# Norm scale moved into the qkv eviction, fills of v ahead of the sets, both columns ahead of choice: three edits in an eight-layer kernel

## The chip, the cores and the metric

The kernel runs on one core of one Trainium2 chip, as one program launched once. The metric is the time of one execution on the device, in microseconds; lower is better. The engines are called by the names that the profile uses: PE for the matmul engine, PEld for its weight loads, DVE for the vector engine, ACT for the scalar engine, POOL for GpSimd, SP for the engine that issues most transfers. All data is fp32. An fp32 matmul instruction stands in the trace as two records.

## The reference

The input is x of shape (8, 256, 256), that is 2048 tokens of width 256. It goes through four groups of three layers; each group is a half-weighted feed-forward layer, an attention, and the same feed-forward layer again:

```python
x = x + 0.5 * ffn_n(layernorm(x))
x = x + attn_n(layernorm(x))
x = x + 0.5 * ffn_n(layernorm(x))      # n = 0, 1, 2, 3
```

Every feed-forward layer is a shared gated product for all tokens and a choice of 2 of 7, 8, 16 or 8 experts for each token. The second attention (n = 1), which the change touches most, is

```python
qkv = rms(x) @ w_qkv.T; q, k, v = split(qkv)      # x is the normed input
q = rms(q); k = rms(k); w = exp(k)
y = sigmoid(q) * cumsum(w * v) / (cumsum(w) + 1e-6)
u, g = split(y @ w_swiglu.T)
out = x + u * silu(g) @ w_out.T
```

where rms(x) is x times the inverse root of the mean of its squares plus EPS1. Its input is already the layernorm of the stream, so its own rms scale is close to, but not exactly, one. The result contains the normed input once more (the leading x). The third attention (n = 2) is causal softmax attention with 32 heads of width 8 and biases on q, k, v and the output.

## The kernel before, in words

The 2048 tokens are 16 tiles of 128 (`NT`), held in SBUF as `net.x[i]`, and four blocks of four tiles (`NB`). A block is the unit of all stages. The function `moments` (L292) takes a block's mean and variance with four pairs of bn_stats and bn_aggr on DVE (L298, L299) and a square root on ACT (L269 and L270 in `root`). `norm_rows` (L304) inverts the root and forms minus mean times scale on DVE (L306, L308), and writes the normed rows on ACT (L310) into `net.rows`, one buffer for all 16 tiles. `to_columns` (L277) transposes four row tiles on PE (L284, two banks with the tag "t") and copies the halves out, the first on DVE and the second on ACT (both L285), to `hT`, which the products read.

A feed-forward layer is an object of the class `Sparse`. `norm` writes its rows, `columns` (L817) transposes them and computes the routing logits (L829, turned back at L843, copied out by DVE at L841 and L850), `choose` (L864) picks two experts by some twenty small DVE operations that end with L898, and `place` (L923) counts with two small matmuls (L932, L933), computes each token's slot on DVE (L937 to L952, the slot's cast is L950), and has POOL scatter the block's rows to DRAM, `sent`, one indirect transfer to a tile (L961). The experts fetch their tokens from there as `got` and turn them on PE (L1077). Their results go back with indirect transfers (`back`), and `combine` (L1141, eight DVE operations a block at L1149, reading `mine`) adds them to x. The shared product runs in `glu_steps`: matmuls L351 into banks "up", an activation L355 or L358 on ACT, a product L364 on DVE, matmuls L369 into "y", and the addition L376 to x on DVE.

`Sparse.body` (L1230) is one pass through such a layer. It calls `arrange` with the blocks that are still to be routed, and a generator `beside` that hands out pieces of the shared product: `beside(7)` means, run pieces until their amounts sum to 7. Inside `arrange` PE's order is written by hand: PE issues what the code issues, in that order. The other engines' instructions are put in order by the compiler's scheduler from estimated costs. After the pass over the experts, `body` runs the rest of the shared product and the combines, and after each block's combine calls `after(j)`, which for a first pass is `normed` (L1971): it writes the normed rows of that block for the attention that follows.

An attention then leaves some blocks to the layer behind it. It routes the others itself while its last work runs, and returns the rest: blocks 2 and 3 after the first and the fourth attention, block 3 after the second and the third. These are the blocks that `arrange` gets in the second pass of each layer. In the first pass of the first layer it gets all four, in the first passes of the others none.

The second attention is `attn1` (L1337). For each block it calls `attn1_front` (L1320): POOL adds the normed rows to x (L1328), ACT squares the rows with a sum (L1330), DVE and ACT make the rms scale, DVE scales the rows in place (L1333), and `to_columns` follows. Then for each of four tiles PE computes 768 columns as 512 and 256 (L1356, four banks with the tag "up"), DVE copies both to `qkv` (L1363), and ACT takes the sums of squares of q and k (L1366). These give `r`, the scale of q and k (L270, L275, L1371). After the four blocks comes a scan over the 16 tiles: two exponentials on ACT (`w` L1382, `eq` L1384), a product on POOL (L1385), cumulative sums by matmuls with a triangle and ones (L1389, L1390), and four DVE operations (L1393 to L1397, of which L1395 is a reciprocal).

The third attention is `attn2` (L1635) with the class `HeadTiles` (L1408). Its constructor casts two constants, `eye` (L1432) and `far` (L1430), takes two sets of four zeroed tiles (qs, ks, qm, km; fills on POOL at L1445) and then 16 tiles `v`, filled with ones on POOL (L1454), because one column of each head must be 1. Then for each block q and k are computed (L1655, banks "a" and "b", three each), evicted on ACT with bias (L1657; the scaled bias of q comes from L1646 on DVE), written to DRAM as `qd` and `kd`; the four v products (L1665) go to banks "t" and DVE adds their bias into `v` (L1669). `load(0)` reads the first heads back into set 0, and the scores (L1486) follow. Tiles of these pools lie where tiles of the stage before lay, so that a fill waits until the last reader of what was there is done.

Of the kernel before, what the change touches and what calls it, by code (L numbers as in the profile page):

```python
# [183 lines left out]
class Net:  # L184


    def __init__(self, ctx, tc, io):
        self.tc, self.nc, self.io = tc, tc.nc, io
        nc = self.nc
        self.const = ctx.enter_context(tc.tile_pool(name="const", bufs=1))  # L190
        self.flow = ctx.enter_context(tc.tile_pool(name="flow", bufs=1))
        self.routes = ctx.enter_context(tc.tile_pool(name="routes", bufs=2))
        self.small = ctx.enter_context(tc.tile_pool(name="small", bufs=2))
        self.dram = ctx.enter_context(tc.tile_pool(name="dram", bufs=2, space=DRAM))
        self.psum = None
        self.passes = 0


        self.sent = self.dram.tile([16 * T + 8 * P, ROW], F32, tag="sent", name="sent", bufs=1)
        self.back = self.dram.tile([2 * T + P * max(TILES.values()), D], F32, tag="back", name="back", bufs=1)  # L200
        self.c = {}
        for k in ("ident",):
            self.c[k] = self.constant(self.const, k)
        self.x = []
        self.stream(0, NT // 2)
        for k in ("ids", "prio7", "base7", "ones", "below", "later4"):
            self.c[k] = self.constant(self.const, k)
        self.router = {"f0": self.load(self.const, "f0_r")}
        self.f0_b = self.row(self.const, "f0_b")

        self.rows = self.flow.tile([P, NT, ROW], F32, tag="rows", name="rows")
        self.hT = [None] * NB

    def stream(self, lo, hi):

# [71 lines left out]

    def norm_block(self, j, tiles):

        self.norm_rows(j, tiles, *self.moments(j))  # L290

    def moments(self, j):  # L292

# [468 lines left out]
class Sparse:  # L762
# [389 lines left out]

    def arrange(self, blocks, beside):

        for j in blocks[:2]:
            self.norm(j)
        if 0 < len(blocks) < NB:
            beside(7)
        for i, j in enumerate(blocks):
            self.columns(j)  # L1160
            self.choose(j)
            if i + 2 < len(blocks):
                self.norm(blocks[i + 2])
            beside(5)
            self.place(j)
# [151 lines left out]
EPS1 = 1.1920929e-07  # L1317


def attn1_front(net, j):  # L1320


    nc = net.nc
    tiles = net.row_tiles(j)
    ss = net.small.tile([P, 4], F32, tag="ss", name="ss")
    for q in range(4):
        x = net.x[4 * j + q]
        nc.gpsimd.tensor_tensor(x, x, tiles[q], ALU.add)  # L1328
        junk = net.small.tile([P, D], F32, tag="sq", name="sq", bufs=1)
        nc.scalar.activation(junk, tiles[q], AF.Square, accum_out=ss[:, q : q + 1])  # L1330
    net.rstd(ss, ss, 1.0 / D, EPS1)
    for q in range(4):
        nc.vector.tensor_scalar(tiles[q], tiles[q], ss[:, q : q + 1], None, ALU.mult)  # L1333
    net.hT[j] = net.to_columns(tiles, j)


def attn1(net, w, then):  # L1337
    nc, tc = net.nc, net.tc
    with tc.tile_pool(name="a1", bufs=2, reuse_waits="tile") as pool:
        triu = net.constant(pool, "triu")  # L1340
        ones = net.c["ones"]
        up = net.load(pool, "a1_up", parts=4)
        dn = net.load(pool, "a1_dn", parts=2)
        wqkv = w["a1_qkv"]
        with tc.tile_pool(name="a1k", bufs=1, reuse_waits="tile") as keep:
            qkv, rr = [], []
            for j in range(NB):
                attn1_front(net, j)
                hT = net.hT[j]
                r = keep.tile([P, 8], F32, tag=f"r{j}", name=f"r{j}")  # L1350
                for q in range(4):
                    t = keep.tile([P, 768], F32, tag=f"qkv{4 * j + q}", name=f"qkv{4 * j + q}")
                    for lo, hi in ((0, 512), (512, 768)):
                        ps = net.bank("up", 4)
                        for k in range(KD2):
                            nc.tensor.matmul(  # L1356
                                ps[:, : hi - lo],
                                lhsT=hT[:, k, q * P : (q + 1) * P],
                                rhs=wqkv[:, k, lo:hi],
                                start=(k == 0),  # L1360
                                stop=(k == KD2 - 1),
                            )
                        nc.vector.tensor_copy(t[:, lo:hi], ps[:, : hi - lo])  # L1363
                    for n in range(2):
                        junk = pool.tile([P, D], F32, tag="junk", name="junk")
                        nc.scalar.activation(  # L1366
                            junk, t[:, n * D : (n + 1) * D], AF.Square, accum_out=r[:, 4 * n + q : 4 * n + q + 1]
                        )
                    qkv.append(t)
                net.rstd(r, r, 1.0 / D, EPS1)  # L1370
                nc.vector.tensor_scalar(r[:, 0:4], r[:, 0:4], -1.0, None, ALU.mult)  # L1371
                rr.append(r)

            yT = []
            for j in range(NB):
                outs = []
                last = None
                for q in range(4):
                    i = 4 * j + q
                    t, r = qkv[i], rr[j]  # L1380
                    w = pool.tile([P, 2, D], F32, tag="w", name="w", bufs=3)
                    nc.scalar.activation(w[:, 1, :], t[:, D : 2 * D], AF.Exp, scale=r[:, 4 + q : 5 + q])  # L1382
                    eq = pool.tile([P, D], F32, tag="eq", name="eq")
                    nc.scalar.activation(eq, t[:, 0:D], AF.Exp, scale=r[:, q : q + 1])  # L1384
                    nc.gpsimd.tensor_tensor(w[:, 0, :], w[:, 1, :], t[:, 2 * D :], ALU.mult)  # L1385
                    cum = net.bank("up", 4)
                    wf = w.rearrange("p a d -> p (a d)")
                    if i % 2:
                        nc.tensor.matmul(cum, lhsT=ones, rhs=last, start=True, stop=False)  # L1389
                    nc.tensor.matmul(cum, lhsT=triu, rhs=wf, start=(i % 2 == 0), stop=True)  # L1390
                    last = wf

                    nc.vector.tensor_scalar(eq, eq, 1.0, None, ALU.add)  # L1393
                    nc.vector.scalar_tensor_tensor(eq, cum[:, D:], 1e-6, eq, ALU.add, ALU.mult)
                    nc.vector.reciprocal(eq, eq)  # L1395
                    y = pool.tile([P, D], F32, tag="yv", name="yv", bufs=5)
                    nc.vector.tensor_tensor(y, cum[:, :D], eq, ALU.mult)  # L1397
                    outs.append(y)
                yT.append(net.to_columns(outs, j))
        with tc.tile_pool(name="a1g", bufs=2, reuse_waits="tile") as mids:  # L1400
            for j in range(NB):
                net.glu_block(mids, yT[j], j, up, dn, AF.Silu, 1.0)
                if j < NB - 1:
                    then.front(j)
    return [NB - 1]


class HeadTiles:  # L1408
# [15 lines left out]
    def __init__(self, net, pool, keep):  # L1424
        self.net, self.nc, self.pool = net, net.nc, pool
        nc = self.nc

        far = net.constant(keep, "far")
        self.far = keep.tile([P, 4, P], BF16, tag="far16", name="far16")
        nc.vector.tensor_copy(self.far, far.unsqueeze(1).to_broadcast([P, 4, P]))  # L1430
# [16 lines left out]
            self.sets.append(t)  # L1447
        self.qd = net.dram.tile([256, T], F32, tag="qd", name="qd", bufs=1)
        self.kd = net.dram.tile([256, T], F32, tag="kd", name="kd", bufs=1)

        self.v = []
        for i in range(NT):
            t = keep.tile([P, 32 * self.V + 32], F32, tag=f"v{i}", name=f"v{i}")
            nc.gpsimd.memset(t, 1.0)  # L1454
            self.v.append(t)
        self.p0, self.p1, self.mx, self.o = {}, {}, {}, {}

    def load(self, b):
# [176 lines left out]
def attn2(net, wt, then):  # L1635
    nc, tc = net.nc, net.tc
    with (
# [9 lines left out]
        for j in range(NB):  # L1647
# [12 lines left out]
                ht.load(0)  # L1660
            for q in range(4):
                i = 4 * j + q
                ps = net.bank("t")
                for k in range(KD2):
                    nc.tensor.matmul(  # L1665
                        ps[:, :D], lhsT=hT[j][:, k, q * P : (q + 1) * P], rhs=wt["v"][:, k, :], start=(k == 0), stop=(k == KD2 - 1)
# [283 lines left out]
def kernel(ctx: ExitStack, tc: tile.TileContext, io, out: bass.AP):  # L1950
# [36 lines left out]
    for n in range(4):  # L1987
        if n:
            w = layers[n].w
            with stage() as net.psum:  # L1990
                following.body([], normed)
            now = experts(n, w)
            with stage() as net.psum:
                left = (attn1, attn2, attn3)[n - 1](net, w, now)
        if n < 3:
            layers[n + 1] = Layer(net, n + 1).load()
            following = experts(n + 1, layers[n + 1].w, first=True)
        with stage() as net.psum:
            if n < 3:
                now.body(left, then=following)  # L2000
            else:
                now.body(left, store)
        layers[n].stack.close()
# [18 lines left out]
```

## Time and profile before

| | us |
|---|---|
| median of 3 runs (3299.05 to 3299.37) | 3299.24 |
| the profiled execution | 3293.35 |
| its span, first to last instruction | 3291.6 |
| PE busy | 2953.8 (90%) |
| PEld busy | 2035.0 (62%) |
| DVE busy | 1766.9 (54%) |
| POOL busy | 1348.2 (41%) |
| ACT busy | 1222.3 (37%) |
| mean granted clock of PE | 0.942 |

The profile is that of one execution, and its instructions lie between 0 and 3291.6 us. The engines' shares are means over the whole span; the stages differ. The six stretches in which the lines of the change run:

| stretch | us | PE busy | DVE busy | ACT busy | POOL busy | granted clock |
|---|---|---|---|---|---|---|
| routing after the first attention | 1213 to 1262 | 20.43 | 23.68 | 13.57 | 19.45 | 0.73 |
| second attention, first block | 1568.7 to 1591 | 15.27 | 21.00 | 15.06 | 7.04 | 0.81 |
| second attention, other blocks | 1591 to 1627 | 34.98 | 18.30 | 25.61 | 4.06 | 0.96 |
| routing after the second attention | 1837 to 1889 | 50.72 | 21.76 | 14.96 | 7.70 | 1.00 |
| third attention, products | 2150 to 2230 | 62.41 | 37.08 | 24.66 | 29.87 | 0.87 |
| routing after the third attention | 2552 to 2587 | 20.02 | 16.57 | 12.07 | 11.10 | 0.79 |
| routing after the fourth attention | 3049 to 3123 | 70.19 | 29.81 | 21.61 | 24.78 | 0.96 |

In the lines of a timeline, the columns are the start and the time in microseconds, the engine, the line of the code, the operation, the tiles it writes and reads with their shapes, how many records are put together, and in brackets the idle time of that engine just before and what ended it.

### The profile page before, as it was taken

Reading aid. Unit: us, or ns where it says so; the run is one execution under the profiler, and the core shown is the slowest. Engines: PE = TensorE matmul, PEld = TensorE weight load, DVE = VectorE, ACT = ScalarE, POOL = GpSimd, SP = SyncE. Lnnn points to the kernel's source line nnn. Section 1 sums busy time; section 2 is a strip of 40 time slices with the busy share of each in tenths; the row PEclk is TensorE's granted clock in tenths of the full one; section 3 lists DMA queues with packets and bytes.
Section 4 is the critical chain, followed back from the end, with each engine's and each line's share of the span. In section 5 each row is a group of like instructions: output and inputs, shape, how many; then the busy total and the mean of one; then the engine's idle time right before and its main releaser. Section 6 shows DMA issues by size and latency. Waiting matters only on the chain. (4 is left out here: it accounts for less than half of the span.)

```text
span 3291.6 us, 44235 instructions
## 1 busy us (share of the span) xinstructions
PE 2953.8 (90%) x14069; PEld 2035.0 (62%) x14098; DVE 1766.9 (54%) x4710; ACT 1222.3 (37%) x2694; POOL 1348.2 (41%) x1616
## 2 busy tenths in 40 slices
PE   5769999999999986799899997879998779988999
PEld 3647777777777755466446674645555556755575
DVE  4646566666666566643753336445775453354433
ACT  3233223323233242333622243434775452335331
POOL 3436666666766534333201133541334442302330
PEclk9889999999999987899999998887998899998999
DMA  7333333233311023433100334541112552312132
GB/s 216 118 105 83 100 100 99 84 89 102 89 42 38 27 95 120 139 115 99 52 4 23 120 96 150 155 121 46 33 35 69 183 175 75 101 40 68 59 94 90
DMA packets 203339, 300.01 MB, mean 91 GB/s; under 512 B 30200, under 2 KB 156792, under 8 KB 201752
## 3 DMA queue, kind: packets, MB, share of 16 engines
q1 hardware_dynamic: 174840, 219.67, 23.1%
q0 software_dynamic: 28272, 77.51, 6.5%
q8 instruction: 118, 1.93, 0.3%
q14 instruction: 109, 0.89, 0.1%
HBM read 178.78 MB, written 118.04 MB: 90 GB/s over the span
## 5 line engine op out<-in xcount | busy, mean ns | idle before, releaser
L961 POOL DMA_INDIRECT back<-res,d_dest x326 | 313.4, 961 | 517.1 <-ACT res L1126 418.6
L961 POOL DMA_INDIRECT sent<-rows,r_slot x256 | 250.7, 979 | 492.8 <-issue 237.3
L1092 PE MATMUL up<-f_eup,hs 128*128 x1304 | 355.3, 396 | 10.6 <-issue 9.2
L351 PE MATMUL up<-hT,f_up 128*128 128x512 f32 x704 | 328.4, 621 | 1.5 <-DVE r_run L952 0.9
L1122 PE MATMUL y<-f_edn,midT 88*128 (+1 forms) x964 | 262.9, 382 | 0.0
L1092 PEld LDWEIGHTS up<-f_eup,hs 128*128 128x128 f32 x1304 | 213.3, 195 | 54.9 <-issue 15.4
L351 PEld LDWEIGHTS up<-hT,f_up 128*128 128x128 f32 x704 | 140.4, 202 | 160.5 <-issue 156.1
L369 PE MATMUL y<-f_dn,mid 128*128 128x256 f32 x768 | 194.7, 406 | 46.4 <-DVE x L376 30.3
L1079 DVE COPY hs<-t 128x256 f32<-128x256 f32 x326 | 138.0, 423 | 168.6 <-PE t L1077 167.6
L696 PE MATMUL up<-vo,hT 128*128 128x256 f32 x1024 | 226.7, 379 | 0.0
L577 DVE TENSOR_TENSOR o<-up,mid 128x512 f32<-128x512 f32 x192 | 132.6, 691 | 162.8 <-ACT mid L576 162.6
L696 PEld LDWEIGHTS up<-vo,hT 128*128 128x128 f32 x1024 | 194.3, 190 | 40.0 <-issue 15.0
L576 ACT COPY mid<-up 128x256 f32<-128x256 f32 x192 | 71.4, 372 | 394.0 <-PE up L572 392.1
L556 POOL TENSOR_TENSOR ddq<-d0q,d2q 128x256 f32<-128x256 f32 x128 | 217.5, 1728 | 0.0
L369 PEld LDWEIGHTS y<-f_dn,mid 128*128 128x128 f32 x768 | 151.0, 203 | 92.6 <-DVE x L376 36.5
L364 DVE TENSOR_TENSOR mid<-act,up 128x512 f32<-128x512 f32 x112 | 76.7, 686 | 234.2 <-PE up L351 216.6
L1077 PE MATMUL t<-c_ident,got 128*128 128x128 f32 x652 | 132.4, 287 | 64.8 <-DMA got<-sent 50.2
L1563 POOL TENSOR_SCALAR_AFFINE_SELECT p<-p 128x512 f32<-128x512 f32 (+1 forms) x192 | 93.0, 485 | 228.2 <-ACT p L1546 144.5
L1098 ACT ACTIVATE eact<-up 128x176 f32<-128x176 f32 (+1 forms) x232 | 70.6, 304 | 308.5 <-PE up L1092 293.9
L1122 PEld LDWEIGHTS y<-f_edn,midT 88*128 88x128 f32 (+1 forms) x964 | 158.3, 191 | 15.5 <-ACT midT L1112 1.3
L1506 DVE TENSOR_REDUCE mx<-a 128x2 f32<-128x512 f32 (+1 forms) x192 | 123.8, 688 | 79.8 <-PE a L1505 52.8
L358 ACT ACTIVATE act<-up 128x512 f32<-128x512 f32 x112 | 66.8, 597 | 252.5 <-PE up L351 242.4
(358 smaller groups left out, 6306.7 us busy)
## 6 DMA issues: line engine op xcount, KB each, us to landing
got<-sent SPq DMA_DIRECT2D x326, 129.0 KB
sent<-rows SPq DMA_DIRECT2D x64, 516.0 KB
mine<-back SPq DMA_DIRECT2D x64, 512.0 KB
dbc<-dd SPq DMA_DIRECT2D x64, 384.0 KB
f_eup<-in_f_eup_dram SPq DMA_DIRECT2D x16, 704.0 KB
f_eup<-in_f_eup_dram SPq DMA_DIRECT2D x14, 512.0 KB
f_edn<-in_f_edn_dram SPq DMA_DIRECT2D x8, 704.0 KB
back<-res,d_dest POOLq DMA_INDIRECT x326, 2.4
```

Of the source, the lines that this page charges most:

```text
L351: nc.tensor.matmul(t, lhsT=up[:, c, m, k, :], rhs=hT[:, k, :], start=(k == 0), stop=(k == KD2 - 1))
L369: nc.tensor.matmul(y[:, :D], lhsT=mids[c][:, q * P : (q + 1) * P], rhs=dn[:, c, :], start=(c == 0), stop=(c == nch - 1))
L556: nc.gpsimd.tensor_tensor(dd[:, 2 * f, u], shifted(d0[:, f])[u], d2[:, f], ALU.subtract)
L577: nc.vector.tensor_tensor(o[:, i], sides.rearrange("p (u n) -> p u n", u=2), t.unsqueeze(1).to_broadcast([P, 2, N]), ALU.add,)
L696: nc.tensor.matmul(ps[:, u * 256 : (u + 1) * 256], lhsT=hT[j][:, k, q * P : (q + 1) * P], rhs=vo.vo[:, h, k, :], start=(k == 0), stop=(k = ...
L961: ins = self.nc.gpsimd.indirect_dma_start(out=out, out_offset=bass.IndirectOffsetOnAxis(ap=index, axis=0), in_=in_, in_offset=None).ins
L1077: nc.tensor.transpose(ps[:, k * P : (k + 1) * P], got[:, k * P : (k + 1) * P], self.net.c["ident"])
L1079: nc.vector.tensor_copy(t, ps[:, : KD2 * P].rearrange("p (k t) -> p k t", k=KD2))
L1092: nc.tensor.matmul(ps[:, :ncol], lhsT=hs[:, k, :], rhs=up[:, bass.ds(x, 1), k, :], start=(k == 0), stop=(k == KD2 - 1))
L1122: nc.tensor.matmul(y[:, :D], lhsT=midT[:, c, :], rhs=dn[:, bass.ds(x, 1), c, :], start=(c == 0), stop=(c == parts - 1))
L1506: nc.vector.tensor_reduce(out, by, AX.X, ALU.min, negate=True)
L1563: self.nc.gpsimd.affine_select(out=e, in_=e, pattern=[[0, n], [1, P]], compare_op=ALU.is_ge, fill=0.0, base=0, channel_multiplier=-1)
```

## The change

There are three edits.

The second attention. `attn1_front` is gone. A new function `normed1` takes the place of `normed` in the pass ahead of this attention. It normalizes the block as before and computes the rms scale `ss1` from the variance and the scale that the norm has already, without squaring the rows: two products, a scaling and a reciprocal on DVE, a square root on ACT. The rows are left unscaled. They are transposed as they are, and the scale is applied where the products are evicted, for each token's partition: the 512 half by a tensor_scalar on DVE, the 256 half by a copy with scale on ACT. POOL's additions of the rows to x stand behind the loop over the four blocks.

The third attention. The 16 tiles of `v` and their fills come first in the constructor, ahead of the sets, in the program and in the pool's memory. The v products use the banks "a" and "b" alternately, with q and k, in place of "t".

The blocks that an attention leaves. Where `arrange` gets some but not all blocks, it asks for an amount of 4 of the shared product in place of 7, and computes the columns and logits of all of these blocks before it chooses and places the first.

```diff
+def normed1(net, j):
     nc = net.nc
-    tiles = net.row_tiles(j)
-    ss = net.small.tile([P, 4], F32, tag="ss", name="ss")
-    for q in range(4):
-        x = net.x[4 * j + q]
-        nc.gpsimd.tensor_tensor(x, x, tiles[q], ALU.add)
-        junk = net.small.tile([P, D], F32, tag="sq", name="sq", bufs=1)
-        nc.scalar.activation(junk, tiles[q], AF.Square, accum_out=ss[:, q : q + 1])
-    net.rstd(ss, ss, 1.0 / D, EPS1)
-    for q in range(4):
-        nc.vector.tensor_scalar(tiles[q], tiles[q], ss[:, q : q + 1], None, ALU.mult)
-    net.hT[j] = net.to_columns(tiles, j)
+    mv, rs = net.norm_block(j, net.row_tiles(j))
+    ss = net.ss1[:, 4 * j : 4 * j + 4]
+    nc.vector.tensor_tensor(ss, mv[:, :, 1], rs, ALU.mult)
+    nc.vector.tensor_tensor(ss, ss, rs, ALU.mult)
+    net.rstd(ss, ss, 1.0, EPS1)
...
-                attn1_front(net, j)
-                hT = net.hT[j]
+                tiles = net.row_tiles(j)
+                hT = net.hT[j] = net.to_columns(tiles, j)
...
-                        nc.vector.tensor_copy(t[:, lo:hi], ps[:, : hi - lo])
+                        ss = net.ss1[:, 4 * j + q : 4 * j + q + 1]
+                        if lo == 0:
+                            nc.vector.tensor_scalar(t[:, lo:hi], ps[:, : hi - lo], ss, None, ALU.mult)
+                        else:
+                            nc.scalar.activation(t[:, lo:hi], ps[:, : hi - lo], AF.Copy, scale=ss)
...
+            for i in range(NT):
+                nc.gpsimd.tensor_tensor(net.x[i], net.x[i], net.rows[:, i, 1 : D + 1], ALU.add)
...
     def arrange(self, blocks, beside):
         for j in blocks[:2]:
             self.norm(j)
         if 0 < len(blocks) < NB:
-            beside(7)
+            beside(4)
+            for j in blocks:
+                self.columns(j)
         for i, j in enumerate(blocks):
-            self.columns(j)
+            if len(blocks) == NB:
+                self.columns(j)
             self.choose(j)
...
     def __init__(self, net, pool, keep):
+        self.v = []
+        for i in range(NT):
+            t = keep.tile([P, 32 * self.V + 32], F32, tag=f"v{i}", name=f"v{i}")
+            nc.gpsimd.memset(t, 1.0)
+            self.v.append(t)
...
-        self.v = []
-        for i in range(NT):
-            t = keep.tile([P, 32 * self.V + 32], F32, tag=f"v{i}", name=f"v{i}")
-            nc.gpsimd.memset(t, 1.0)
-            self.v.append(t)
...
-                ps = net.bank("t")
+                ps = net.bank("ab"[q % 2], 3)
...
-                following.body([], normed)
+                following.body([], (lambda j: normed1(net, j)) if n == 1 else normed)
```

## The prediction

> **What bounds the kernel now.** I read the page first. PE is busy 2953.8 of 3291.6 us (90%); no other engine is over 54%. A saving therefore comes from a gap on PE, or from a chain that PE waits for, in the stage where it stands. Next I read the timeline of PE through the six stretches that the diff touches, and beside each one the timelines of the engines that end its gaps. Columns of a timeline: start, time, engine, line, operation, tiles, count, and in brackets the idle time before and what ended it. One fp32 matmul stands in the records as two.
>
> Second attention, its qkv products:
>
> ```profile
> 1567.44 0.69 PE L284 MATMUL t<-c_ident,rows 128*128 128x128 f32 x2 [3.50 <-DVE rows L1333]
> 1568.70 13.31 PE L1356 MATMUL up<-a_qkv,hT 128*128 128x512 f32 x32 [0.57 <-DVE hT L285]
> 1588.96 2.07 PE L284 MATMUL t<-c_ident,rows 128*128 128x128 f32 x8 [6.95 <-DVE r L1371]
> 1591.17 11.98 PE L1356 MATMUL up<-a_qkv,hT 128*128 128x512 f32 x32
> ...
> 1604.55 10.59 PE L1356 MATMUL up<-a_qkv,hT 128*128 128x512 f32 x32 [0.53 <-DVE hT L285]
> 1614.97 1.04 PE L284 MATMUL t<-c_ident,rows 128*128 128x128 f32 x8
> 1616.36 10.59 PE L1356 MATMUL up<-a_qkv,hT 128*128 128x512 f32 x32 [0.34 <-DVE hT L285]
> ```
>
> PE waits 3.50 and 6.95 us for rows that DVE still scales (L1333), queued behind evictions and combines. The products of a block take 10.59 us when PE is warm, 13.31 and 11.98 after those gaps: the granted clock is 0.50 from 1568.7 to about 1573 and from 1589 to 1594, then 1.00.
>
> Third attention, its v products, on PE and on POOL:
>
> ```profile
> 2178.77 1.89 PE L1665 MATMUL t<-a_v,hT 128*128 128x256 f32 x8
> 2187.85 3.70 PE L1665 MATMUL t<-a_v,hT 128*128 128x256 f32 x8 [7.19 <-DVE v L1669]
> ```
>
> ```profile
> 2184.93 2.08 POOL L1445 MEMSET km<- 128x2048 f32 x1
> 2186.96 4.99 POOL L1454 MEMSET v<- 128x320 f32 x16
> ```
>
> The third v product waits for bank t. DVE can't empty it before POOL's first fill of v at 2186.96, the last of POOL's fills.
>
> The stretches where an attention's left blocks are routed differ. After the first attention (blocks 2, 3) and the third (block 3), POOL's scatters end the wait:
>
> ```profile
> 1261.15 0.66 PE L1077 MATMUL t<-c_ident,got 128*128 128x128 f32 x2 [16.76 <-DMA got<-sent]
> ```
>
> ```profile
> 2586.10 1.27 PE L1077 MATMUL t<-c_ident,got 128*128 128x128 f32 x4 [12.11 <-DMA got<-sent]
> ```
>
> After the second (block 3) and the fourth (blocks 2, 3) PE itself is full to 1888.23 and 3122, the scatters being done by 1865 and 3094; every new gap there is paid.
>
> **Second attention.** Removed: per block four squares on ACT (L1330, 0.41 each, 1.64) and four scalings on DVE (L1333, 0.34 each, 1.13 to 1.22). Added: four small DVE operations (0.17 each, 0.7), which give the scale from mv and rs before the rows are written. Moved: four evictions of 256 columns from DVE (0.42) to ACT (0.37 by the PSUM copies of L576); the 512 half stays at DVE (0.69). POOL's 16 additions x+=rows (0.65 to 0.8 each, beside which the combine L1149 takes 5.02 instead of 3.25) no longer stand ahead of the scaling, though in POOL's order they keep about their places.
>
> I place the blocks by DVE's and ACT's order in the changed program. Block 0: transposes may end at 1564.4, but combine(1) (3.25) and a bn_stats still stand ahead of the hT copy, so the products start at 1567.85, 0.85 earlier; the gap is still over 3 us, so 13.3 again, to 1581.15. Block 1: its rows were written by 1574.5, the transposes follow at once; the second hT half is on ACT behind the last tile's eviction and two squares (0.37+0.82+0.57), so products at 1582.9 instead of 1591.17: 8.3 earlier. Now warm: 10.6+1.04+1.4 puts block 2 at 1595.9 instead of 1604.55: 8.65. In block 2 ACT has ahead of its first eviction: w and eq (0.5 each), three table loads (1.28 each), three square roots (0.2 each) and rows(3) (2.07), 7.5 us, to 1603.5. PE has four banks, runs 7 us on them and on what DVE frees, and stands for about 1 us: block 3 at 1609.2 instead of 1616.36, its end at 1619.8 instead of 1626.78. Gain **7.0**. The scan behind it is DVE's (L1395, 1.75 of 2.6 us a tile, 16 tiles) and has the same work, so the 7.0 arrives. Bounds: 11 if ACT never holds PE (7 of idle, 2.7 of block 0's slow clock, 1.4 of block 1's), 3 if ACT's 7.5 holds PE in blocks 1 and 3 as well.
>
> **Third attention.** The 16 fills of v (4.99) go ahead, to 2153.5, where POOL is idle. In exchange the sets lie where the routing's tiles lay: all but one of their eight fills now wait for the last combine (2181.17), in sum some 10.5 us, to about 2191.7. Four v products no longer need bank t but share a and b, so transposes of blocks 1 and 2 (0.6+0.66, 0.15 idle, twice: 2.8) come into the gap. What ends it then is the q eviction on ACT, which waits for DVE's a_bq (L1646, ended 2187.03). That operation took 1.60 and L269 before it 1.34, where such small ones take 0.17 elsewhere; each ended with a fill. By the same fills shifted, eye ends at 2182.3, two more hT copies (0.69) follow, far ends at 2186.0 and a_bq at 2186.9: PE goes on near 2187.9 as before, with 2.8 us of transposes done; I take **2.0**, since ACT's evictions wait for qd and kd transfers near 2218 too. Load(0) went out at 2193.6; set 0 is filled by 2186, which hides its fills. Bounds: 5 gained, if a_bq slips in first; 1.9 lost, if it waits for the last fill (2191.7, 4.7 later, less the 2.8).
>
> The Trainium skill (page "SBUF — State Buffer", section "Who interferes with whom") says that tensor_scalar and casts in a two-port mode and POOL exclude one another for a whole instruction. The trace agrees (1.60 beside a fill). By that rule an operation that comes up just after a fill began loses all of it, fill after fill: that is rival 4 below.
>
> **Left blocks.** beside(7) becomes beside(4): one chunk of shared products (8 records, 3.60 us warm) instead of two ahead of the transposes; each chunk passed over comes later, so its work is neutral on PE.
> - First attention: T(2) waits for rows(2) (1220.9) but comes 4.4 earlier; then all of block 3's columns and choice stand on DVE ahead of place(2), and on PE a chunk stands ahead of the counts L932. The slot index was cast at 1236.19 and the first scatter came 0.77 later; now about 1238.2: **2.0 lost** (0 to 4).
> - Second: the chunk ends at 1841.05, rows(3) at 1843.4: a gap of 2.35 on a full PE; 0.4 of it is won back as the transposes come earlier: **1.9 lost** (1 to 4).
> - Third: the transposes follow rows(3) at 2559.2 and not 2561.98; 0.6 is lost on DVE: **2.2 won** (0 to 3).
> - Fourth: no second chunk covers T(3), which waits for rows(3) (3059.3); about 1 of gap more: **1.0 lost** (-1 to 3).
> Together 2.7 lost (-2 to 11).
>
> On gaps: after 2.21 us of idle (1219.7) the granted clock is still 1.00; after 8.40 (2165.9) it is 0.50, and eight records of L351 take 5.55 (2552.80) instead of 3.60. The Trainium skill ("TensorE: Matmul & The Clock Gate", "Part 1: The HAM clock gate (the "warmup" mystery)") puts the idle time that halves the clock near 3.4 us. The first attention's new gap ahead of T(2) is of that size; by that rule the chunk behind it would be slow and the slot index later.
>
> **Sum.** -7.0 -2.0 +2.7 = -6.3 us. The profiled execution took 3293.35 (span 3291.6, 1.75 around it), 5.9 less than the median 3299.24. On its own time the change gives 3287.0; on the median, which is what I predict, **3292.9**. A measurement of this kernel tells about 0.2%, 6.6 us, from no change.
>
> **Rivals.**
> 1. ACT never holds PE in the qkv loop: 11 instead of 7 in the second attention, -10.3, 3289. For it: most of ACT's table loads were in the loop before, and it kept pace (25.6 busy of 36 us). Against it: evictions now stand behind them, which DVE's did not.
> 2. ACT becomes the bound there: 3 instead of 7, -2.3, 3297. For it: ACT needs 12 to 13 us a block (2 to 3 loads, rows 2.07, squares 3.28, evictions 1.5, w and eq 1 to 2, hT 0.57), PE 11.6.
> 3. Slower: gaps ahead of the left blocks' transposes put PE on the half clock. Place: the chunk behind each T. Price: 1.95 a chunk (5.55-3.60) beside the gap itself: 4 after the first attention, 4 after the second, 3 after the fourth, and nothing won after the third: 11. It decides from 9 us (7.0+2.0); then +2, 3301, and over 0.2% slower only if ACT gives back as well. Against it: the gap of 2.21 left the clock at 1.00.
> 4. The third attention's gap stays, as a_bq's wait takes the place of the fill's: the fills behind the last combine now last to 2191.7. It restarts 4.7 later with 2.8 of transposes done, 1.9 lost instead of 2.0 won: -2.4, 3297.
>
> **How the numbers follow.** Forecast 0.42 (3288 to 3297, its half on either side of 3292.6, the 0.2% line); rival 1 0.20, faster; rival 2 0.16 and rival 4 0.12, same; rival 3 0.10, 0.07 of it slower. Faster 0.21+0.20, with 0.01 for more: 0.42; same 0.21+0.16+0.12+0.02: 0.51; slower 0.07. The range takes in rival 1 with the third attention's 5 (3286) and most of rival 3: 3285 to 3302.
>
> **What would show it.** Right: block 1's products at about 1583 with no gap of 6.95 and at 10.6 us, a stand of about 1 us in block 2 before an ACT eviction, the scan 7 us earlier against the stage's start; POOL's fills of v near 2153 and the v gap ended by ACT's qk with two blocks of transposes in front; a gap near 2.3 us ahead of T(3) after the second attention. Wrong: DVE waiting for POOL's fills to 2191, block 3's products less than 4 us earlier, a clock of 0.50 behind a left block's transposes, or the first scatter after the first attention not later. The sum fails most easily in the order of ACT's queue.

## The result

| | us |
|---|---|
| before, median of 18 runs (3290.85 to 3309.68) | 3299.3 |
| changed, median of 18 runs (3282.68 to 3299.42) | 3294.93 |
| ratio, with its 95% interval | 0.9984 (0.9977 to 0.9992) |
| profiled execution of the changed kernel, and its span | 3291.47, 3289.6 |

The forecast was 3292.9 with a range of 3285 to 3302. The change makes the kernel 4.4 us faster by the medians; the interval of the ratio reads 2.6 to 7.6.

Single executions of either kernel scatter by 17 to 19 us, so the two spans (3291.6 and 3289.6) say little. What can be read is a stretch: the time between the same two matmuls in two profiles, in which an offset from earlier drops out.

| stretch | before | changed | difference | forecast |
|---|---|---|---|---|
| blocks left by the first attention: shared product to first turned got | 47.27 | 49.47 | +2.2 | +2.0 |
| second attention: its last y products to the scan's first matmul | 76.60 | 70.38 | -6.2 | -7.0 |
| the same, to the glu's L351 behind the scan | 122.56 | 117.08 | -5.5 | -7.0 |
| block left by the second attention | 50.62 | 54.32 | +3.7 | +1.9 |
| third attention: shared product ahead of it to its last q, k or v product | 78.32 | 76.15 | -2.2 | -2.0 |
| the same, to the shared product behind the attention | 402.83 | 398.75 | -4.1 | -2.0 |
| block left by the third attention | 33.30 | 31.53 | -1.8 | -2.2 |
| blocks left by the fourth attention | 72.48 | 72.01 | -0.5 | +1.0 |

With the second attention taken to its glu and the third to its end, the six differences sum to -5.9 us, taken from the unrounded times. The spans differ by only 2.0: the code outside these stretches took 3.9 us longer in this one execution (more on that in the last section).

The second attention on PE, with the columns as before: start, time, what ran, idle time before it and what ended it. Kernel after:

```profile
1560.47 5.49 PE L372 MATMUL y<-f_dn,mid 128*128 128x256 f32 x12 [6.89 <-DVE x L379]
1565.75 1.44 PE L285 MATMUL t<-c_ident,rows 128*128 128x128 f32 x8
1570.57 13.66 PE L1357 MATMUL up<-a_qkv,hT 128*128 128x512 f32 x32 [3.38 <-DVE hT L286]
1584.06 1.04 PE L285 MATMUL t<-c_ident,rows 128*128 128x128 f32 x8
1585.54 10.56 PE L1357 MATMUL up<-a_qkv,hT 128*128 128x512 f32 x32 [0.44 <-ACT junk L1371]
1595.93 1.04 PE L285 MATMUL t<-c_ident,rows 128*128 128x128 f32 x8
1598.55 7.98 PE L1357 MATMUL up<-a_qkv,hT 128*128 128x512 f32 x24 [1.58 <-ACT junk L1371]
...
1610.56 10.56 PE L1357 MATMUL up<-a_qkv,hT 128*128 128x512 f32 x32 [0.44 <-ACT junk L1371]
```

The gap of 6.95 us between blocks 0 and 1 is gone, and block 1 takes 10.56 instead of 11.98. But the first line is a gap that grew: PE's last y products waited 4.50 us before and wait 6.89 now. Kernel before, on PE and on DVE:

```profile
1557.69 5.49 PE L369 MATMUL y<-f_dn,mid 128*128 128x256 f32 x12 [4.50 <-DVE x L376]
```

```profile
1557.21 0.75 DVE L376 SCALAR_TENSOR_TENSOR x<-y,x 128x256 f32<-128x256 f32 x2
```

The reason stands on DVE and ACT in the same stretch of the kernel after:

```profile
1557.99 0.17 DVE L270 TENSOR_SCALAR ss<-ss 128x4 f32<-128x4 f32 x1
1559.93 0.18 DVE L276 RECIPROCAL ss<-ss 128x4 f32<-128x4 f32 x1 [1.77 <-ACT ss L271]
1560.02 0.72 DVE L379 SCALAR_TENSOR_TENSOR x<-y,x 128x256 f32<-128x256 f32 x2
```

```profile
1557.72 2.07 ACT L313 ACTIVATE rows<-x,mr,rs 128x256 f32<-128x256 f32 x4 [0.44 <-DVE mr L311]
1559.71 0.19 ACT L271 ACTIVATE ss<-ss 128x4 f32<-128x4 f32 x1
```

ACT takes the root of the new scale behind the four rows (2.07). DVE's reciprocal waits 1.77 for it, and queued behind the reciprocal are the additions x<-y that empty PE's banks. They begin 9.45 us after the stretch's first y product (1560.02 less 1550.57), before the change 7.03 (1557.21 less 1550.18).

The third attention of the kernel after on PE, and POOL's fills:

```profile
2175.73 1.03 PE L1673 MATMUL b<-a_v,hT 128*128 128x256 f32 x4
2176.59 1.04 PE L285 MATMUL t<-c_ident,rows 128*128 128x128 f32 x8
2178.30 1.09 PE L285 MATMUL t<-c_ident,rows 128*128 128x128 f32 x8 [0.68 <-ACT hT L286]
2183.54 2.08 PE L1673 MATMUL a<-a_v,hT 128*128 128x256 f32 x4 [4.14 <-ACT qk L1665]
```

```profile
2149.19 4.98 POOL L1439 MEMSET v<- 128x320 f32 x16
...
2177.06 0.95 POOL L1459 MEMSET ks<- 128x1024 f32 x1 [6.85 <-DVE x L1152]
...
2179.78 1.80 POOL L1459 MEMSET km<- 128x2048 f32 x1
2181.53 1.22 POOL L1459 MEMSET qs<- 128x1024 f32 x1
...
2185.36 1.80 POOL L1459 MEMSET km<- 128x2048 f32 x1
```

The fills of v are done early, the transposes of two blocks stand in the old gap, and what ends the rest of it is ACT's eviction of q. PE goes on 37.9 us after the shared product, exactly as before (2187.85 less 2149.97 there, 2183.54 less 2145.63 here), with the transposes of two blocks already done.

### The profile page after: what moved, and what is told of

It reads as the page before. It is cut to its first block, busy times and chain, and to the rows that moved or that the text cites. A ratio compares the mean times of both kernels' runs of the same rounds, so it can differ in the third digit from the quotient of the medians.

```text
span 3289.6 us, 44211 instructions
## 1 busy us (share of the span) xinstructions
PE 2963.5 (90%) x14098; PEld 2037.0 (62%) x14098; DVE 1747.3 (53%) x4686; ACT 1213.5 (37%) x2673; POOL 1344.5 (41%) x1616
```

## The experiments

By the record's numbers they ran on three chips (e1 to e4 on one, e5 to e8 on the next, e9 to e12 on the last). The kernel before takes 3375.55, 3375.65 and 3375.72 us on them (medians of 35, 21 and 19 runs) and not 3299.3, so only ratios and stretches are compared. Part of the difference stands on DVE: its waits of over 2 us for which the profile names no engine (it writes `remote`) sum to 15 to 61 us in the twelve profiles, to 2.1 and 0 in the first pair.

### e1 to e4: each edit alone, and the first two together

e1 is the changed kernel with the second and third edit undone, e2 and e3 the kernel before with one edit each. e4 undoes only the third:

```diff
-            beside(4)
-            for j in blocks:
-                self.columns(j)
+            beside(7)
         for i, j in enumerate(blocks):
-            if len(blocks) == NB:
-                self.columns(j)
+            self.columns(j)
```

> The first edit alone: normed1 and the scale in the eviction; the third attention and the left blocks as before. Stretches are measured between the same matmuls of a profile, so that an offset from elsewhere drops out. Theory A (from the two profiles): the second attention gains 5 to 6 us from its last y products to its glu products (122.6 before, 117.1 in the changed kernel), and nothing else moves: 3293 to 3294 where before is 3299. In its gap ahead of the last four y products DVE waits some 2.4 us longer than before, for a square root that ACT computes behind four rows. Rival B: that longer gap is only a matter of when a slow clock window fell, and the gap will be near 4.5 again, the gain 7 or more: 3292 or less. Rival C: the gain is an accident of one profile: no change.

Measured: 3367.91 us, ratio 0.9981 (0.9971 to 0.9991). To the scan 68.24 us, to the glu's L351 behind the scan 114.76 (122.56 before): 7.8 gained. The gap ahead of the last y products is 6.88 again. So the longer gap is no accident, against rival B; the gain is larger than A's 5 to 6 nevertheless, because less of the half clock (0.50) fell on it. The y products behind the gap took 4.73 instead of 5.49 and block 0 took 12.28 instead of 13.66, together the 2.1 us by which the scan comes earlier than in the changed kernel. Rival C falls.

> The second edit alone: fills of v first, v products in banks a and b. Theory A: the stretch from the shared product ahead of the third attention to the one behind it is 3 to 5 us shorter (402.8 before, 398.8 in the changed kernel): 3295 to 3296. Rival B: 2 us, as forecast, the rest being luck with the clock: 3297. Rival C: the fills that now follow the last combine hold DVE, and nothing is won: 3299.

Measured: 3372.49, ratio 0.9994 (0.9981 to 1.0007): by itself not told from no change. The products' part took 75.18 us. The whole stretch took 407.18 us against 407.96 in e1 and 408.97 in e3, which lack the edit: less than A said. Single profiles of this stretch differ by more than that (below), so it is inconclusive alone.

> The third edit alone: beside(4), all columns ahead of choice and place. Theory A: it costs 3 to 4 us in all: +2 after the first attention (47.3 us from the shared product to the first turned got), +2 to +4 after the second (50.6), -2 after the third (33.3), 0 after the fourth (72.5): 3302 to 3303. Rival B: the half clock found behind the transposes after the second attention (granted 0.50 from 1840 to 1843) is a matter of where a clock window fell and will be absent in other profiles: +1.5 there, so +1 to +2 in all: 3300 to 3301.

Measured: 3379.61, ratio 1.0011 (1.0000 to 1.0023): slower, as A and B both said. By the ratio it is 3.7 us, A's amount, but the interval, 0 to 7.8, holds B's 1 to 2 as well. After the second attention the stretch took 53.05 (+2.4, as A said). The granted clock stayed at 1.00 there, as B said.

> The changed kernel with the third edit undone (arrange as before). Theory A: the third edit was a loss of 3 to 4 us, so this is the best of the combinations: 3289 to 3291 where before is 3299. Rival B: the third edit costs 1 or less: 3293 to 3295, as the changed kernel.

Measured: 3364.79, ratio 0.9968 (0.9953 to 0.9983). The gains of e1 and e2 add up (7.6 and 3.1 by the medians, 10.8 together), and the ratio without the third edit is lower than with it (0.9984 in the first pair). Rival B, a cost of 1 or less, is not excluded by this run: e12, which has the third edit as well, came to 0.9975, and the two intervals overlap. Against B stand e3 and the stretches.

### e5 and e6: the root ahead of the rows

```diff
-    mv, rs = net.norm_block(j, net.row_tiles(j))
+    mv, rs = net.moments(j)
+    nc.vector.reciprocal(rs, rs)
...
-    net.rstd(ss, ss, 1.0, EPS1)
+    net.root(ss, ss, 1.0, EPS1)
+    mr = net.small.tile([P, 4], F32, tag="mr", name="mr")
...
+    nc.vector.reciprocal(ss, ss)
```

> The first edit alone, with one thing other than in e1: normed1 takes the square root of the rms scale ahead of the four rows on ACT, not behind them, so that the reciprocal on DVE, behind which the additions L376 stand in DVE's order, does not wait for the rows. Theory A: the gap ahead of the last four y products goes from 6.9 us back to about 4.5, the products of block 0 start 2 us earlier, and the second attention from its last y products to the scan takes 2 to 3 us less than in e1 (68.2 us where block 0 ran warm, 70.4 where it ran on the half clock). Rival B: the gap returns in front of block 0 as a wait for the hT copy behind the combine, since that combine waits for its data anyway: no change against e1.

Measured: 3366.45, ratio 0.9970 (0.9953 to 0.9987), whose interval overlaps that of e1. To the scan it took 70.83 us, with block 0 on the half clock (13.57), against 70.38 in the changed kernel with the same. PE in e5:

```profile
1590.74 5.49 PE L372 MATMUL y<-f_dn,mid 128*128 128x256 f32 x12 [5.32 <-DVE x L379]
...
1600.83 13.57 PE L1363 MATMUL up<-a_qkv,hT 128*128 128x512 f32 x32 [3.47 <-DVE hT L286]
...
1616.71 7.20 PE L1363 MATMUL up<-a_qkv,hT 128*128 128x512 f32 x20 [1.43 <-DVE rs L1330]
1624.36 3.90 PE L1363 MATMUL up<-a_qkv,hT 128*128 128x256 f32 x12 [0.46 <-DVE qkv L1372]
...
1631.01 2.85 PE L1363 MATMUL up<-a_qkv,hT 128*128 128x512 f32 x8 [1.88 <-DVE hT L286]
```

The gap fell by 1.6 us (DVE's reciprocal now waits 0.21 instead of 1.77), but the scheduler put DVE's other work in another order, and waits for DVE of 1.43, 0.46 and 1.88 came up in blocks 1 and 2. My theory A, 2 to 3 us, failed: the wait went, and what it gave was taken back, later than rival B said.

> e5 with the second edit added and the third left out: the version that the runs so far point to. Theory A: 2 us below the changed kernel without the third edit, a ratio near 0.996 to 0.997 (that one had 0.9968, the changed kernel 0.9984). Rival B: if the wait for the root is worth nothing, 0.997 to 0.998.

Measured: 3360.73, ratio 0.9962 (0.9947 to 0.9976), within A's range, but not told from e4's 0.9968. To the scan 70.53 us, where e4 took 67.48 with block 0 at the full clock.

### e7: all columns first, but beside(7)

> One half of the third edit alone: all columns ahead of choice, but beside(7) as before. Where one block is left this is the order of before, so the stretches after the second and third attention should take 50.6 and 33.3 us. Theory A: after the first attention it costs most of what the whole edit costs, since place(2) stands behind block 3's columns and choice; after the fourth nothing. The other half, 7 to 4, is what costs 2.4 to 3.7 after the second attention and wins 1 to 2 after the third. Rival B: the columns' order is the cost after the second attention too: over 52 us there.

Measured (one run): 50.62 and 33.50 us after the second and third attention, as A said: there the cost and the gain come from the 4. After the first attention 48.13. The unchanged order took 47.8 to 49.5 in nine profiles of these chips, so A's cost of the order is not there. After the fourth the stretch took 80.97, where nine without the edit took 83.86 to 86.63 and the two with all of it 89.63 and 89.79. The first pair took 72 there. On these chips DVE stands in this stretch for waits named `remote` (in e12 4.85, 5.32 and 6.67 us), of which the first pair has none; what they wait for, and how the edit moves them, is open.

### e8: both halves of an eviction on DVE

```diff
-                        if lo == 0:
-                            nc.vector.tensor_scalar(t[:, lo:hi], ps[:, : hi - lo], ss, None, ALU.mult)
-                        else:
-                            nc.scalar.activation(t[:, lo:hi], ps[:, : hi - lo], AF.Copy, scale=ss)
+                        nc.vector.tensor_scalar(t[:, lo:hi], ps[:, : hi - lo], ss, None, ALU.mult)
```

> The first edit alone, with both halves of an eviction on DVE, none on ACT. Theory A: ACT's queue, in which the evictions stand behind table loads and rows, held the second block's products 1.0 to 1.6 us ahead of their start and the hT copies 0.4 to 1.6 behind squares; that goes, and DVE, busy about half of that stretch, takes 0.42 a tile more: 1 to 2 us less than e1 to the scan's start. Rival B: DVE's combines (3.3 us, in order) hold the evictions as they did before the change: 2 or more us longer than e1.

Measured: 3371.49, ratio 0.9986 (0.9974 to 0.9998), not told from e1's 0.9981, and 70.99 us to the scan, 2.8 more than e1. The clock explains none of it: block 0 took 10.59 here and 12.28 in e1, block 1 12.28 here and 10.56 in e1. PE in e8:

```profile
1600.27 10.59 PE L1354 MATMUL up<-a_qkv,hT 128*128 128x512 f32 x32 [3.74 <-DVE hT L286]
...
1614.33 12.28 PE L1354 MATMUL up<-a_qkv,hT 128*128 128x512 f32 x32 [2.60 <-DVE hT L286]
...
1629.52 10.59 PE L1354 MATMUL up<-a_qkv,hT 128*128 128x512 f32 x32 [2.04 <-DVE hT L286]
```

Rival B holds: the hT copies stand behind DVE's combines and evictions, and PE waits 2.60 and 2.04 for them. ACT's waits, which this was to remove, are shorter (1.04 and 1.57 in e4). In this stretch a third of the evictions on ACT is worth about 3 us.

### e9 and e10: the halves of the second edit

e9 moves only the fills of v, e10 only the banks of the v products.

> One half of the second edit alone: the fills of v first, the v products in banks t as before. Read is the time from the shared product ahead of the third attention to its last q, k or v product: 78.2 to 79.3 us without the edit, 75.2 to 76.2 with all of it. Theory A: the third v product no longer waits for a fill, but for DVE, which empties bank t only behind the casts and the bias: most of the idle 7.2 us stays, and transposes that need bank t cannot come into it: 77 to 79. Rival B: the fills were all of it: 75 to 76.

Measured (one run): 77.36 us to the last product, between the two groups. The gap ahead of the third v product was 5.31 instead of 7.19 and still ended by DVE's addition into v: A's mechanism, with about 1.5 us won.

> The other half alone: v products in banks a and b, the fills of v last as before. Theory A: transposes of the next two blocks come into the gap, as in the whole edit, but DVE's addition into v waits for the last fills, near the same moment as before: 75.5 to 77 for the same stretch. Rival B: without the early fills nothing moves, 78 to 79.

Measured (one run): 76.25, as A said. PE in e10, which has the transposes in the gap and its end from ACT, as in the changed kernel:

```profile
2222.23 1.04 PE L284 MATMUL t<-c_ident,rows 128*128 128x128 f32 x8
...
2230.18 2.08 PE L1665 MATMUL a<-a_v,hT 128*128 128x256 f32 x4 [4.38 <-ACT qk L1657]
```

So in one profile each the banks alone win 2.6 of the 3.0 us that the whole edit wins here, and the fills alone 1.5.

### e11 and e12: only the winning part of the third edit, beside the changed kernel

```diff
-            beside(4)
-            for j in blocks:
-                self.columns(j)
+            beside(4 if self.n == "f2" else 7)
```

> First and second edit as in the changed kernel; of the third only its winning part: beside(4) in the layer behind the third attention, beside(7) and the old order of columns elsewhere. Theory A: the second attention's and the third's gains with 1 to 2 us more after the third attention: a ratio of 0.996 to 0.997, 3 to 6 us below the changed kernel. Rival B: what is won after the third attention is lost again behind it: 0.997 to 0.998.

Measured: 3357.38, ratio 0.9946 (0.9928 to 0.9965), a larger gain than A's 0.996. The block left by the third attention took 31.73 us; nine profiles without the 4 took 32.90 to 34.00, two others with it 32.26 (e3) and 32.89 (e12).

> The changed kernel itself, beside e11 on one chip, with another profile of it. Theory A: 0.998 to 0.999, above e11 by the third edit's cost of 3 to 4 us; after the second attention the stretch takes 53.0 us if no slow clock window falls on its transposes and 54.3 if one does. Rival B: no higher than e11, the third edit costs nothing.

Measured: 3365.18, ratio 0.9975 (0.9960 to 0.9990), 7.8 us above e11 by the medians, against B and more than A's 3 to 4. Together with e3 that makes the third edit, outside the layer behind the third attention, a loss on these chips, but its size is not firm. e11 differs from e4 in that one layer only, whose stretch gains 1.2 us, and yet its ratio stands 0.0022 (7.4 us) below e4's, so part of e11's lead is likely scatter. After the second attention the stretch took 54.31 us, with the clock at 0.50 behind the transposes, as A said. e11 is the fastest version found by its median; its interval overlaps those of e4 and e6.

## Why the prediction was right

The total came nearer than its parts, which is partly luck. The second attention gave 1.5 us less than forecast and the left blocks 1.0 less, while the third attention gave 2.1 more in this pair, and later profiles don't bear those 2.1 out.

**The second attention** was right in its mechanism and a little large. Forecast were 7.0; 6.2 arrived at the scan and 5.5 behind it. Two terms were off. First, "the products start at 1567.85, 0.85 earlier" failed: measured from the last y products, block 0 starts 1.5 us later than before, 2.3 behind the forecast. The term that I left out is the reciprocal's wait for a root that ACT takes behind the rows, and the additions queued behind it on DVE; I had counted the four new DVE operations at 0.7 and not their wait. Second, "stands for about 1 us" in block 2 did not come: blocks 1 and 2 run through in 10.6 and 10.8, and 1.3 to 1.5 of the 2.3 is won back by the scan. Block 0's 13.66 is close to what I forecast (13.3). With the same code it took 12.28 in e1, e11 and e12 and 10.59 in e4, and there the stretch to the scan took 67.5 to 68.3, which is 8.3 to 9.1 less than before. Another 0.7 went in the scan, where PE once waits 0.97 for POOL's product, which itself stood 11.67 us for ACT's exponential; POOL's additions x+=rows were done by then, in about their old places, as forecast. Rivals 1 and 2 both fall: ACT ended three gaps of PE (0.44, 1.58 and 0.44), so it did hold PE, but it was no bound. (The items that I gave for ACT under rival 2 add to 11 to 13 us a block, not 12 to 13.)

**The third attention** came out as worked: PE restarts where it did, with the transposes done. In six profiles with the edit the products end 75.2 to 76.2 us after the shared product, in the six without it 78.2 to 79.3: 3.0 on the means (75.85 and 78.86), against a forecast of 2.0. Rival 4, DVE held by the fills, did not come, though the fills did hold it. The fills stand above; DVE of the kernel after:

```profile
2180.01 1.85 DVE L1444 CAST far<-c_far 128x512 bf16<-128x512 f32 x1
...
2181.86 0.91 DVE L1654 TENSOR_SCALAR a_bq<-a_bq 128x2 f32<-128x2 f32 x1
```

The cast ended just after the fill of km that began at 2179.78 (1.80), and the bias came through at 2182.77, just after the fill of qs that began at 2181.53 (1.22), while POOL filled on to 2187. The Trainium skill ("SBUF — State Buffer", "Who interferes with whom") says that whoever issues first has the shared ports for the whole instruction and the other blocks. The trace agrees with that, and it shows that each of these operations lost at most the fill it met: DVE got in between two fills. Over the whole attention the edit's gain is less sure: 4.1 in the first pair of profiles, and 2.1 between the means of five profiles each on the other chips (407.2 with it, 409.4 without; single profiles overlap).

**The left blocks** were forecast at +2.7 and gave +3.7. (The lower bounds of its four terms add to -3, not -2.) After the first attention, "the slot index was cast at 1236.19 ... now about 1238.2: 2.0 lost" is what the pair shows (slot index and first scatter 2.3 later), but later profiles leave less of it: without the edit's 4, the first scatter comes 23.1 to 25.0 us after the shared product in eleven profiles, with all of the edit 25.3 to 25.7 in three. On the means about 1 us is left. The clock is mixed up in it. Four of the eleven ran at 1.00 from 3 to 18 us after the shared product's start and have 23.1 to 23.7; the others had 3.4 us at 0.50 in that time and have 24.2 to 25.0; the three with the edit all had 10.2 us at 0.50 from about 8 us on. What the order costs by itself there is open. The third attention's block was right (-1.8; -1.3 between the means of all profiles). The fourth's was not worth its 1.0 in the pair; on the other chips the two profiles with the edit took 3 us longer than the longest of nine without, and why is open (e7). The term that was mis-sized is the second attention's, 1.9 forecast and 3.7 measured. PE in the kernel before, where nothing interrupts it, and in the kernel after:

```profile
1837.61 7.03 PE L351 MATMUL up<-hT,f_up 128*128 128x512 f32 x16
1844.48 1.04 PE L284 MATMUL t<-c_ident,rows 128*128 128x128 f32 x8
```

```profile
1836.92 0.33 PE L285 MATMUL t<-c_ident,rows 128*128 128x128 f32 x1 [0.80 <-ACT rows L313]
...
1838.39 0.77 PE L285 MATMUL t<-c_ident,rows 128*128 128x128 f32 x5 [0.16 <-ACT rows L313]
1839.50 1.02 PE L832 MATMUL t<-hT,f_r 128*32 128x128 f32 x16 [0.35 <-DVE hT L286]
```

There is no one gap of 2.35, but PE is thinly used for 5 us. This shows in the granted clock of that stretch (the third number from the end of a line; the first time behind the window's length is PE's busy time), for the kernel after and then for e3, which has the same code there:

```profile
1838.00:1840.00 2.00, 1.49 (x18) 0.89 (x22) 0.69 (x1) 1.13 (x3) 0.00 (x0) 0.90 1.02 425
1840.00:1842.00 2.00, 1.61 (x14) 0.67 (x7) 0.80 (x5) 1.07 (x1) 0.00 (x0) 0.50 0.95 307
1842.00:1844.00 2.00, 2.00 (x5) 0.97 (x4) 1.79 (x13) 1.59 (x2) 0.00 (x0) 0.74 0.66 152
```

```profile
1865.00:1867.00 2.00, 1.33 (x11) 0.74 (x14) 0.69 (x1) 1.14 (x3) 0.00 (x0) 1.00 1.03 431
1867.00:1869.00 2.00, 1.58 (x19) 0.80 (x20) 0.75 (x4) 1.49 (x2) 0.00 (x0) 1.00 0.96 348
```

At 0.50 the stretch takes 54.32 (54.31 in e12), at 1.00 it takes 53.05: 2.4 for the order itself and 1.3 for the clock. My row, "the gap of 2.21 left the clock at 1.00", argued against rival 3 and misled me: a clock can be halved without any one long gap. In the 3.41 us before the drop at 1839.62 PE was busy for 1.87, with no gap over 0.80; in e3 the windows lie otherwise against the same code, hold 2.67 and 2.51, and the clock stayed at 1.00. Rival 3's sign, which I had named as one of being wrong, came at more places than this one: 0.50 behind a left block's transposes also stands after the first attention (10.2 us in all three profiles with the edit) and, on the other chips, after the fourth (10.2 us in e3 and e12, 3.4 to 6.8 in those without all of it). Its price of 11 was too large: the four stretches lost 3.7 in the pair.

## What to carry to other kernels

When a small chain is moved onto an engine that works its queue in order, as DVE did here, price its wait as well as its operations, and look at what is queued behind the waiting one: here 0.7 us of operations cost 2.4 us of a gap. Moving a wait away need not shorten a stage, since the scheduler reorders the rest (e5). Take an edit of several parts apart before keeping it: the third one here won in one layer and lost in others, and without the losing places the kernel was 7.8 us faster by the medians of one chip, a size that is not firm.

## What the runs showed of the hardware

PE's granted clock changes on a grid of its own. In the trace's record of the clock, nearly all intervals at 0.50 last 3.4, 6.8, 10.2, 13.7 us and so on, multiples of 3.41, and the grid lies otherwise against the program in each execution. The Trainium skill ("TensorE: Matmul & The Clock Gate", "Part 1: The HAM clock gate (the "warmup" mystery)") gives a free-running window of 3413 ns, and the trace agrees. The same code then costs different times: block 0 of the second attention 13.66 us in one execution and 10.59 in another. The runs did not settle how much of the 17 to 19 us of scatter between executions this makes, nor what the 3.9 us are that the rest of the code took longer in the first profile of the changed kernel; a difference of 1 or 2 us in one stretch of one pair of profiles is no finding until a third profile repeats it.
